# The GRU's r and z gates put into free halves of PSUM banks

## The chip, the cores and the metric

The kernel runs on one core of a Trainium2 chip. Five engines work side by side, each on its own list of instructions in order: TensorE (PE in the profile; its weight loads are PEld), VectorE (DVE), ScalarE (ACT), GpSimd (POOL) and SyncE (SP, which only issues DMAs here). They wait for one another by semaphores. There are two on-chip memories: SBUF, and PSUM with eight banks, into which TensorE writes its products. The metric is the device time of one execution in microseconds.

## The reference

A GRU runs over 128 time steps for a batch of 64 rows with 512 features, and its output is added to the input. All is float32. What one step does:

```
comb   = concat(x_t, h)
z      = sigmoid(comb @ Wz + bz)
r      = sigmoid(comb @ Wr + br)
h_cand = tanh(concat(x_t, r * h) @ Wh + bh)
h_new  = (1 - z) * h + z * h_cand
h_next = tanh(h_new @ Wp + bp)  if (t + 1) % 4 == 0 and t < T - 1  else  h_new
out[:, t] = x_t + h_new
```

The step needs the h of the step before, so the 128 steps form one chain. Only the products of x_t with the upper halves of the weights can be made ahead of time.

## The kernel before, in words

**Layout.** The state h is a tile of 128 partitions by 2 by 128. The 64 batch rows are split into two halves of 32 (index s_, the tile's middle dimension), and the 512 features into four quarters that lie on four groups of 32 partitions. A gate (`gate`, line 210) is 16 small products, each of which the profile shows as two MATMUL rows, so 32 per gate. They are written into the first half of a PSUM bank. There are three such banks, `rec_r`, `rec_z` and `rec_h` (line 154), each a tile of `[P, S, 2, J]`. Index 0 of the second dimension is the gate's own half. In `rec_r` the other half is used by the projection (`gate_ps(P_)`, line 158); in `rec_z` and `rec_h` it is free.

**One step.** In order:

1. Gate r on TensorE from the transposed state hT. Four activations on ScalarE (`crossed`, line 225; two for each half s_, as each moves 64 partitions) give r. For each half VectorE makes r*h (line 673) and transposes it into rhT (line 232). ScalarE then seeds the bank for the next step: `seed` copies the x part of the next step's gate, prepared in SBUF tile `cp`, into the gate's half of the bank, so that the next gate adds to it.
2. Gate z on TensorE, four activations, and on VectorE one instruction for keep = (z - 1) * h (line 686). Then `seed(Z, t + 1)`. In a projection step ScalarE also copies the projection's bias into `rec_r`.
3. Gate h from rhT, four tanh activations giving cand; for each half VectorE multiplies cand by z (line 718, in place), then subtracts keep to get h_new (line 728), and transposes it into hT. Then `seed(H_, t + 1)`.
4. Every fourth step a projection: a fourth gate, four tanh activations, two transposes.
5. GpSimd adds h_new to the input tile (line 794), and every fourth step SP writes four steps out.

**Work put between.** The products with x are made by a fast scheme with fewer multiplications that combines two groups of four steps at a time. It leaves TensorE a queue of units, each four small products (eight MATMUL rows), and `fill(n)` takes n units off that queue. `PLACES` (line 574), with `HEAD` and `TAIL` for the first and last steps, says how many units go ahead of gate h, after gate h, and after the projection. Some units end with work on other engines: ScalarE copies a PSUM bank to SBUF (line 468), VectorE adds a PSUM tile to an SBUF tile (lines 485 to 495), and GpSimd combines the results, by `add` (line 526) and `with_bias` (line 531), into `cp`. GpSimd also makes sums of the transposed x (lines 301 to 333). Since the batches span two groups of four steps, the schedule repeats every eight steps.

**Order and waits.** The order on each engine is the order of the program. The framework adds the waits: one instruction waits for another where they touch the same data. VectorE, ScalarE and GpSimd all take work in order, so an instruction that waits holds up what stands behind it.

Where the tiles of the change lie before: r, z and cand are SBUF tiles with two buffers each (r and cand share the tag "r"). Each of the four VectorE instructions named above (673, 686, 718, 728) thus reads two SBUF tiles.

Of the kernel before, what the change touches and what calls it, by code (L numbers as in the profile page):

```python
# [9 lines left out]
F32 = mybir.dt.float32  # L10
# [8 lines left out]
def kernel(  # L19
# [14 lines left out]
    nc = tc.nc  # L34
    B, T, D = x.shape
    H = h0.shape[1]
    P = 128
    S = 2
    V = B // S
    NQ = P // V  # L40
    J = H // NQ
# [6 lines left out]
    R, Z, H_ = range(3)  # L48
# [13 lines left out]
    two = ctx.enter_context(tc.tile_pool(name="two", bufs=2))  # L62
# [90 lines left out]

    rec = [ps_c.tile([P, S, 2, J], F32, name=f"rec_{n}") for n in "rzh"]
    P_ = 3

    def gate_ps(i):
        return rec[0][:, 1] if i == P_ else rec[i][:, 0]

# [50 lines left out]
    def gate(i, lT, w):  # L210
        for k in range(K):
            products(
                gate_ps(i), lambda h: lT[:, h, ts(k, V)], lambda c: quarters(w)[:, c, k]
            )
# [10 lines left out]
    def crossed(dst, h, ps, func):  # L225
        for d in range(2):
            nc.scalar.activation(  # L227
                dst[ts(d, 2 * V), h, :], ps[ts(h, 2 * V), d, :], func
            )

    def turn(dst, src):
        nc.vector.transpose(out=dst, in_=src)  # L232

    def new_T(tag, name):
        return two.tile([P, S, P], F32, tag=tag, name=name)
# [374 lines left out]
    for t in range(T):  # L610
# [56 lines left out]
            outer_u2(odd - 2)  # L667
        rh = two.tile([P, S, J], F32, tag="rh", name=f"rh_{t}")
        rhT = new_T("rhT", f"rhT_{t}")
        r = two.tile([P, S, J], F32, tag="r", name=f"r_{t}")  # L670
        for s_ in range(S):
            crossed(r, s_, gate_ps(R), AF.Sigmoid)
            nc.vector.tensor_mul(rh[:, s_, :], r[:, s_, :], h[:, s_, :])  # L673
# [5 lines left out]
        join(0)  # L679

        gate(Z, hT, wh[Z])
        z = two.tile([P, S, J], F32, tag="z", name=f"z_{t}")
        keep = two.tile([P, S, J], F32, tag="keep", name=f"keep_{t}")
        for s_ in range(S):
            crossed(z, s_, gate_ps(Z), AF.Sigmoid)
# [9 lines left out]
        if prop:  # L695
            nc.scalar.copy(gate_ps(P_), bias_p)
        if last:
# [13 lines left out]
        gate(H_, rhT, wh[H_])  # L711
        h_new = two.tile([P, S, J], F32, tag="h", name=f"h_{t}")
        hT = None if last else new_T("hT", f"hT_{t}")
        cand = two.tile([P, S, J], F32, tag="r", name=f"c_{t}")
        for s_ in range(S):
            c = cand[:, s_, :]
            crossed(cand, s_, gate_ps(H_), AF.Tanh)
            nc.vector.tensor_mul(c, c, z[:, s_, :])  # L718
            if last:
                o = xr[g][:, j, s_, :]  # L720
                nc.vector.tensor_add(o, c, o)  # L721
                (nc.sync, nc.scalar)[s_].dma_start(
                    out=out[ts(s_, V), t, :].rearrange("b (q n) -> q b n", q=NQ),
                    in_=o,
                )
                continue
        if not last:
            nc.vector.tensor_sub(h_new, cand, keep)  # L728
            turn(hT, h_new)
        if t < T - 2:  # L730
            seed(H_, t + 1)
# [6 lines left out]
        if prop:  # L738
            gate(P_, hT, wp)
            h = two.tile([P, S, J], F32, tag="hprop", name=f"hprop_{t}")  # L740
            hT = new_T("hT", f"hpT_{t}")
            for s_ in range(S):
                crossed(h, s_, gate_ps(P_), AF.Tanh)
                turn(hT[:, s_, :], h[:, s_, :])
# [112 lines left out]
```

## Time and profile before

| | |
|---|---|
| median of 3 runs | 1597.43 us (1591.34 to 1598.39) |
| profiled execution | 1592.18 us, span 1590.4 us |
| mean granted TensorE clock | 0.956 |
| PE busy | 1377.0 us, 87% of the span |
| DVE busy | 980.6 us, 62% |
| POOL busy | 910.1 us, 57% |
| ACT busy | 750.7 us, 47% |
| DMA | mean 40 GB/s |

How to read the lines that follow. A group row has the line, engine and operation, the tiles as out<-in, the shapes, the count, then the busy time in us with the mean of one instruction in ns, and last the idle time of the engine ahead of these instructions with what ended it. A row of the waits names who waited for whom, the total in us, how often, and the longest. A timeline row has the start in us, how long it took in us, the engine, line and operation, and in brackets the idle time of the engine before it. TensorE is called busy also where its matmuls only follow each other slowly, and its matmuls overlap, so the starts of matmuls tell more than the busy time.

### The profile page before, as it was taken

How to read it: one execution, taken by the hardware profiler on the slowest of the kernel's cores; microseconds unless marked ns; L12 is line 12 of the kernel's file. 1: busy time of each engine (PE TensorE's matmuls, PEld its weight loads, DVE VectorE, ACT ScalarE, POOL GpSimd, SP SyncE). 2: the span in 40 equal slices, each digit the busy share in tenths (PEclk: the TensorE clock that was granted, in tenths of full speed). 3: DMA queues.
4: the chain of work that ended last, by engine and by line, in shares of the span. 5: the costliest groups of instructions: out<-in, count | busy, mean ns of one | idle time of the engine just before them, and what ended most of it. 6: DMA issues, size and time to landing. Idle time of an engine off the chain costs nothing. (4 is left out here: it accounts for less than half of the span.)

```text
span 1590.4 us, 59768 instructions
## 1 busy us (share of the span) xinstructions
PE 1377.0 (87%) x26024; PEld 923.5 (58%) x26024; DVE 980.6 (62%) x1909; ACT 750.7 (47%) x2401; POOL 910.1 (57%) x1030
## 2 busy tenths in 40 slices
PE   6688898889898898898889889889898889889797
PEld 2255665656565565665656566566665656566464
DVE  0356566766757566666766666676566666666643
ACT  0134444545545454554545455455454445544444
POOL 2276665756656575666756555575666656566420
PEclk7799999999999999999999999999999999999999
DMA  2311110111111011110111111011110111111021
GB/s 99 108 55 42 33 38 16 42 42 42 29 29 48 22 42 29 48 36 16 45 38 43 29 35 49 16 42 39 46 29 20 50 29 43 29 42 29 8 83 28
DMA packets 114147, 63.13 MB, mean 40 GB/s; under 512 B 12604, under 2 KB 109116, under 8 KB 113884
## 3 DMA queue, kind: packets, MB, share of 16 engines
q1 hardware_dynamic: 113176, 58.97, 13.2%
q8 instruction: 204, 3.34, 0.9%
q14 instruction: 59, 0.48, 0.1%
q10 hardware_dynamic: 452, 0.20, 0.0%
q0 software_dynamic: 256, 0.14, 0.0%
HBM read 42.47 MB, written 16.78 MB: 37 GB/s over the span
## 5 line engine op out<-in xcount | busy, mean ns | idle before, releaser
L227 ACT ACTIVATE r<-rec_r 64x128 f32<-64x128 f32 x512 | 139.3, 272 | 411.8 <-PE rec_r L201 405.6
L201 PE MATMUL rec_h<-wh,rhT 128*32 128x256 f32 x4096 | 283.0, 381 | 53.8 <-DVE rhT L232 50.9
L201 PE MATMUL rec_r<-wh,hT 128*32 128x256 f32 x3072 | 211.5, 422 | 107.7 <-DVE hT L232 106.8
L673 DVE TENSOR_TENSOR rh<-r,h 128x128 f32<-128x128 f32 x192 | 140.5, 732 | 173.3 <-ACT r L227 173.3
L201 PEld LDWEIGHTS rec_h<-wh,rhT 128*32 128x32 f32 x4096 | 144.2, 110 | 163.2 <-DVE rhT L232 74.9
L718 DVE TENSOR_TENSOR c<-c,z 128x128 f32<-128x128 f32 x256 | 148.8, 589 | 144.7 <-ACT c L227 142.8
L227 ACT ACTIVATE c<-rec_h 64x128 f32<-64x128 f32 x512 | 139.2, 272 | 206.6 <-PE rec_h L201 200.4
L201 PEld LDWEIGHTS rec_r<-wh,hT 128*32 128x32 f32 x3072 | 103.8, 119 | 193.1 <-DVE hT L232 120.2
L526 POOL TENSOR_TENSOR cp<-mb,mb 128x768 f32<-128x768 f32 x75 | 136.1, 1815 | 119.0 <-DVE mb L495 115.4
L201 PE MATMUL rec_z<-wh,hT 128*32 128x256 f32 x3072 | 199.3, 403 | 0.0
L794 POOL TENSOR_TENSOR xr<-xr,h 128x256 f32<-128x256 f32 x127 | 93.5, 736 | 139.6 <-DVE h L728 139.6
L227 ACT ACTIVATE z<-rec_z 64x128 f32<-64x128 f32 x512 | 139.2, 272 | 51.5 <-PE rec_z L201 40.0
L526 POOL TENSOR_TENSOR mb<-mb,mb 128x768 f32<-128x768 f32 x58 | 108.5, 1870 | 91.1 <-DVE mb L495 91.1
L201 PEld LDWEIGHTS rec_z<-wh,hT 128*32 128x32 f32 x3072 | 110.5, 118 | 76.7 <-issue 23.0
L526 POOL TENSOR_TENSOR cp<-mb 128x768 f32<-128x768 f32 x47 | 88.6, 1886 | 67.6 <-ACT rec_h L369 66.1
L468 ACT COPY cq<-scratch_q 128x384 f32<-128x384 f32 (+1 forms) x214 | 102.4, 479 | 25.0 <-DVE mb L486 20.4
L686 DVE SCALAR_TENSOR_TENSOR keep<-z,h 128x256 f32<-128x256 f32 x96 | 78.7, 819 | 55.2 <-ACT z L227 55.2
L728 DVE TENSOR_TENSOR h<-c,keep 128x256 f32<-128x256 f32 x127 | 103.2, 813 | 12.4 <-DVE c L718 0.5
L531 POOL TENSOR_TENSOR mb<-mb,bias_x 128x768 f32<-128x768 f32 x35 | 64.4, 1839 | 66.6 <-DVE mb L495 66.6
L526 POOL TENSOR_TENSOR cp<-cp,mb 128x768 f32<-128x768 f32 x29 | 52.9, 1824 | 85.0 <-DVE mb L495 83.9
L232 DVE STREAM_TRANSPOSE rhT<-rh 128x128 f32<-128x128 f32 x256 | 79.7, 311 | 8.9
L201 PE MATMUL scratch_r<-tw,s 128*32 128x192 f32 x928 | 73.4, 326 | 0.0
(157 smaller groups left out, 2815.7 us busy)
## 6 DMA issues: line engine op xcount, KB each, us to landing
out_dram<-xr SPq DMA_DIRECT2D x249, 64.0 KB
xr<-in_x_dram SPq DMA_DIRECT2D x248, 64.0 KB
xs<-in_x_dram SPq DMA_DIRECT2D x240, 64.0 KB
wx<-in_L_cond_Wr_dram SPq DMA_DIRECT2D x7, 256.0 KB
wx<-in_L_cond_Wz_dram SPq DMA_DIRECT2D x7, 256.0 KB
wx<-in_L_cond_Wh_dram SPq DMA_DIRECT2D x7, 256.0 KB
wh<-in_L_cond_Wr_dram SPq DMA_DIRECT2D x4, 256.0 KB
wh<-in_L_cond_Wz_dram SPq DMA_DIRECT2D x4, 256.0 KB
```

The lines of the kernel that those rows point to most:

```text
L201: nc.tensor.matmul(ps[part(2 * h + c)], lhsT=lhs(h), rhs=rhs(c), start=start, stop=True, skip_group_check=True,)
L227: nc.scalar.activation(dst[ts(d, 2 * V), h, :], ps[ts(h, 2 * V), d, :], func)
L232: nc.vector.transpose(out=dst, in_=src)
L468: nc.scalar.copy(c[:, :nm], ps[:, :nm])
L526: nc.gpsimd.tensor_add(dst, a, b)
L531: nc.gpsimd.tensor_add(m, m, v.unsqueeze(1).to_broadcast([P, 2, 3 * J]))
L673: nc.vector.tensor_mul(rh[:, s_, :], r[:, s_, :], h[:, s_, :])
L686: nc.vector.scalar_tensor_tensor(out=keep, in0=z, scalar=1.0, in1=h, op0=ALU.subtract, op1=ALU.mult)
L718: nc.vector.tensor_mul(c, c, z[:, s_, :])
L728: nc.vector.tensor_sub(h_new, cand, keep)
L794: nc.gpsimd.tensor_add(xr[g][:, j], xr[g][:, j], h_new)
```

## The change

r and z get no SBUF tile any more: r becomes the free half of bank `rec_h`, z the free half of bank `rec_z`, one place each for all steps. ScalarE's activations for them write to PSUM. cand stays in SBUF under a tag of its own. The product with z is written over z, and the subtraction reads it from there. Each of the four VectorE instructions now has one input in PSUM and one in SBUF. Orders, counts and shapes of the instructions are the same, and so are all DMAs.

```diff
     rec = [ps_c.tile([P, S, 2, J], F32, name=f"rec_{n}") for n in "rzh"]
     P_ = 3
+    r, z = rec[H_][:, 1], rec[Z][:, 1]
...
-        r = two.tile([P, S, J], F32, tag="r", name=f"r_{t}")
         for s_ in range(S):
             crossed(r, s_, gate_ps(R), AF.Sigmoid)
             nc.vector.tensor_mul(rh[:, s_, :], r[:, s_, :], h[:, s_, :])
...
         gate(Z, hT, wh[Z])
-        z = two.tile([P, S, J], F32, tag="z", name=f"z_{t}")
         keep = two.tile([P, S, J], F32, tag="keep", name=f"keep_{t}")
...
-        cand = two.tile([P, S, J], F32, tag="r", name=f"c_{t}")
+        cand = two.tile([P, S, J], F32, tag="c", name=f"c_{t}")
         for s_ in range(S):
-            c = cand[:, s_, :]
             crossed(cand, s_, gate_ps(H_), AF.Tanh)
-            nc.vector.tensor_mul(c, c, z[:, s_, :])
+            c = z[:, s_, :]
+            nc.vector.tensor_mul(c, cand[:, s_, :], c)
...
-            nc.vector.tensor_sub(h_new, cand, keep)
+            nc.vector.tensor_sub(h_new, z, keep)
             turn(hT, h_new)
```

## The prediction

> **What bounds the kernel now.** The page comes first: its engine shares, then its costliest groups, then the list of waits, the durations of single lines, and the timeline.
>
> ```profile
> PE 1377.0 (87%) x26024; PEld 923.5 (58%) x26024; DVE 980.6 (62%) x1909; ACT 750.7 (47%) x2401; POOL 910.1 (57%) x1030
> L673 DVE TENSOR_TENSOR rh<-r,h 128x128 f32<-128x128 f32 x192 | 140.5, 732 | 173.3 <-ACT r L227 173.3
> L718 DVE TENSOR_TENSOR c<-c,z 128x128 f32<-128x128 f32 x256 | 148.8, 589 | 144.7 <-ACT c L227 142.8
> L728 DVE TENSOR_TENSOR h<-c,keep 128x256 f32<-128x256 f32 x127 | 103.2, 813 | 12.4 <-DVE c L718 0.5
> ```
> TensorE is near full, so only time in which it stands still, or runs slowly, can be won. The three VectorE rows look too dear: the list of groups kept apart by shape has 292 ns for a 128x128 product of step 0 (rh<-r,h_init).
>
> ```profile
> PE rec_r L201 <- DVE hT L232: 110.0, 39, 5.0
> PE rec_h L201 <- DVE rhT L232: 50.9, 57, 1.3
> DVE mb L491 <- ACT cq L468: 21.0, 48, 0.6
> ```
> These are rows of the waits (total, times, longest). TensorE waits on VectorE's two transposes, the ends of the two chains around each gate. The third row is needed later.
>
> ```profile
> L495 DVE TENSOR_TENSOR mb<-scratch_y,cq x53: 533/547/550, 108.5 to 1518.2; 128x384 f32<-128x384 f32 x53
> L728 DVE TENSOR_TENSOR h<-c,keep x127: 424/427/1974, 73.8 to 1577.3; 128x256 f32<-128x256 f32 x127
> L673 DVE TENSOR_TENSOR rh<-r,h x192: 248/450/1626, 81.9 to 1581.5; 128x128 f32<-128x128 f32 x192
> ```
> Single lines, minimum/median/maximum in ns. L495 adds a PSUM tile to an SBUF tile and never leaves 533 to 550. L728 and L673, two SBUF inputs, reach 1974 and 1626. The timeline shows what they meet:
>
> ```profile
> 812.64 1.95 POOL L526 TENSOR_TENSOR mb<-mb,mb 128x768 f32<-128x768 f32 x1 [4.04 <-DVE mb L495]
> 813.20 1.54 DVE L718 TENSOR_TENSOR c<-c,z 128x128 f32<-128x128 f32 x1 [0.29 <-ACT c L227]
> ...
> 814.55 1.85 POOL L531 TENSOR_TENSOR mb<-mb,bias_d 128x768 f32<-128x768 f32 x1
> 814.85 1.83 DVE L728 TENSOR_TENSOR h<-c,keep 128x256 f32<-128x256 f32 x1
> ...
> 817.22 3.35 PE L201 MATMUL rec_r<-wh,hT 128*32 128x256 f32 x32 [2.65 <-DVE hT L232]
> ```
> Each two-SBUF VectorE instruction that starts inside a GpSimd instruction ends just after it. TensorE stands 2.65 us, and then the gate takes 3.35 us where it takes 1.91 elsewhere:
>
> ```profile
> core 0: us, PE busy (x) PEld busy (x) DVE busy (x) ACT busy (x) POOL busy (x), PEclk, DMA share, GB/s
> 615.70:627.70 12.00, 9.35 (x204) 6.16 (x197) 8.45 (x15) 5.74 (x18) 7.81 (x9) 1.00 0.01 3
> 627.70:643.10 15.40, 11.64 (x212) 7.38 (x216) 10.19 (x17) 5.74 (x18) 9.25 (x10) 0.87 0.12 35
> 643.10:656.30 13.20, 13.14 (x240) 9.59 (x242) 5.69 (x16) 6.45 (x22) 5.18 (x8) 0.89 0.01 3
> ```
> After the two long stalls of a period the granted clock falls to half for 3.4 us; hence 0.87 and 0.89 over those steps.
>
> **The change, part by part.** Undisturbed durations are 292 (rh, c·z), 420 (h) and 425 ns (keep). What all instances take above these is 97.5 (rh) + 76.0 (c·z) + 49.9 (h) + 42.6 us (keep) = 266 us. With one operand in PSUM I expect this to vanish, as for L485 to L495. How much of it TensorE sees needs the steps. The schedule repeats every eight steps (u is step minus 3, modulo 8); from 211.9 to 1445.4 us it runs 13 such periods, 94.88 us each. From the timeline I took, for each u, the mean time from the first gate-r matmul to the last gate-h matmul's start, A, and from there to the next step's first matmul, B:
>
> u: A, B now -> expected
> 0: 7.70, 6.56 -> 5.75, 6.40
> 1: 6.31, 3.20 -> 6.08, 3.20
> 2: 6.28, 5.64 -> 6.28, 2.96
> 3: 8.20, 6.74 -> 6.94, 2.96
> 4: 6.67, 6.40 -> 5.75, 6.40
> 5: 7.13, 2.94 -> 7.13, 2.94
> 6: 6.46, 3.04 -> 5.75, 3.04
> 7: 7.12, 4.50 -> 5.75, 4.40
> sum: 94.89 -> 81.73
>
> How the right side comes out. A gate takes 1.73 us from its first matmul to that of the next, a queue unit 0.325 us, and 1.53 us lie between first and last start of gate h, so TensorE alone needs A = 2 x 1.73 + 0.325 x units + 1.53: 6.28 and 6.94 with 4 and 6 units (u 2, 3). With no unit or one, the chain through r decides. In the undisturbed steps 125 to 127 rhT is ready 3.80 us after the first matmul, and the last gate-h matmul starts 1.59 later.
>
> **New wait on r.** r now lies in gate h's bank. ScalarE writes its second half while VectorE would read the first. The waits row of L491 says how such a pair goes: it reads scratch_q and cx, not what the copy at L468 writes, and yet starts 33 ns after that copy (a reader of the same bank) ends. So I take it that the second pair of activations waits for the first product. Now: two activations 0.56, 0.03 to the product, 0.29, 0.31 transpose, with the second half overlapping, 1.81 in all. Then: 0.56 + 0.03 + 0.28 + 0.09 (the gap from L486 to the copy that waits for it) + 0.56 + 0.03 + 0.28 + 0.03 + 0.31 = 2.17, or 0.36 more. That gives 3.80 + 0.36 + 1.59 = 5.75 for u 0, 4, 6, 7. In u 1, after the conditional projection, r starts later (rhT ready at 4.12 in step 124) and A is 6.08. Queued behind the waiting activation on ScalarE are seed R (0.38) and z; z could start 1.93 us after gate r instead of 1.80, which keep and h outlast. The bound below is no wait: 0.36 less in these five steps, to TensorE's own limit.
>
> [...]
>
> **B.** The undisturbed chain c, product, subtraction, transpose takes 2.47 us, after 0.38 for the last matmul and 0.11 of hand-overs: 2.96. Eight units cover 0.2 + 8 x 0.325 = 2.80, so 0.16 remains of the 2.84 and 3.94 lost in u 2 and 3, and the clock no longer drops, which is the 1.26 in A of u 3 and part of u 4. In u 1 and 7 TensorE waits for ScalarE's copy of a bank (L468); that stays.
>
> **Edits costed at nothing.** keep is read from z's bank, so the copy that seeds it (seed Z) waits for keep, 0.46 us; the bias copy of a projection step and the L468 copies queue behind it. Cover: gate h's matmuls, as ScalarE sits idle 206.6 us before c (1.6 per step). Without the cover it is at most 0.46 us x 127 = 58 us. Single buffers for r and z make nobody wait: h of step t is read before gate r of t+1 can start. No DMA moves; SP's and GpSimd's orders stay. GpSimd's 58 us per period fit 81.7. **Activations into PSUM:** 128x256 copies take 377 ns into PSUM and 374 out, so 0. **c·z writes PSUM in place:** no row. Below, the 279 ns of the fastest L718; above, a second pass over 128 elements at 1.03 ns (349 to 547 ns for 192 more): 132 ns each, 0.26 us in six of eight steps, 25 us. I take 0: the nearest row, L495, shows PSUM traffic at the pace of SBUF rows.
>
> [...]
>
> **Sum.** 13 x 13.16 = 171 us. Before 211.9 us: stalls ahead of steps 2, 5, 6, 7 of 1.75 + 2.61 + 2.66 + 3.76, half-clock gates 6.2, late gates h of steps 9 and 10 2.1, less 2 for the new wait: 17. After 1445.4: 12 by the same reckoning, with 0.36 lost in each of the last five steps. Together 200. The profiled execution took 1592.18 us (span 1590.4), 0.3% under the median of 1597.43: 1392.
>
> **Rivals.**
> (a) r is not serialized: 80 steps x 0.36 = 29 us better, 1363. Against it: L491's wait.
> (b) In-place writes or PSUM activations are slower: 25 us for c·z, or 0.1 us per r activation, 0.4 x 80 = 32: 1417 to 1424.
> (c) c·z still collides, as it alone has SBUF first and PSUM second; every PSUM+SBUF row has them the other way round. Of the 13.2 us per period some 4 to 5 come back: about 1450.
> (d) The change doesn't do what it says: GpSimd delays VectorE whatever the operands. Then the 0.36 us costs 29 us, and seed Z behind the stretched keep (2.9 and 2.4 us after z in u 0 and 7) delays c by 0.5 us a period, 7 us: 1628, slower. It decides when less than a sixth of the stretch goes (36 us of cost against 200 + 29 of gross gain). Against it: L495's 550 ns maximum in a kernel with GpSimd busy 57%.
> (e) The denser schedule meets a new wait, GpSimd's cp or ScalarE's copies: half a microsecond a step, 1455.
>
> **How the numbers follow.** Mine 0.60, a 0.12, b 0.10, c 0.07, d 0.05, e 0.06. Mine alone spans 1370 to 1415 (errors of 0.15 us a step). The range leaves out d, half of c and e, and the fastest part of a: 1355 to 1450. Faster by over 0.5% (8 us, about what can be told here): 0.94; same 0.01; slower 0.05.
>
> **What would show it.** L673, L718, L728, L686 with maxima within 20% of their minima; TensorE's wait for hT from 110 to under 30 us; the clock 0.98 or more; a gap between the second and third r activation of about 0.4 us; keep ahead of seed Z. A c·z row still reaching 1.5 us means (c); all four, (d). The forecast fails if r's hand-over costs over a microsecond, or if other waits take up what VectorE gives back.

## The result, and the profile after

The changed kernel takes 1395.21 us (median of 4 runs, 1394.73 to 1395.70) where the kernel before takes 1596.33 (median of 4). The ratio is 0.8744, 95% interval 0.8723 to 0.8766. The profiled execution has a span of 1392.7 us and a mean granted clock of 0.983 (before 0.956).

The page of the changed kernel, its engine shares and the group of the r*h product. The product's mean was 732 ns:

```profile
PE 1324.7 (95%) x26024; PEld 924.6 (66%) x26024; DVE 733.7 (53%) x1909; ACT 728.3 (52%) x2401; POOL 887.4 (64%) x1030
L673 DVE TENSOR_TENSOR rh<-rec_h,h 128x128 f32<-128x128 f32 x192 | 56.0, 291 | 173.0 <-ACT rec_h L228 173.0
```

VectorE lost 247 us of busy time with the same 1909 instructions. TensorE lost 52 us with the same matmuls and stands at 95% of the span; by an estimate from the granted clocks (0.044 x 1590 us against 0.017 x 1393) up to 46 us of that come from fewer matmuls at half clock.

Single lines of the changed kernel (minimum/median/maximum ns); the lines of keep, of the product with z and of h are one lower than before, those of the helpers one higher:

```profile
L717 DVE TENSOR_TENSOR rec_z<-c,rec_z x256: 285/297/298, 73.1 to 1388.0; 128x128 f32<-128x128 f32 x128
L727 DVE TENSOR_TENSOR h<-rec_z,keep x127: 424/425/427, 74.0 to 1379.3; 128x256 f32<-128x256 f32 x127
L673 DVE TENSOR_TENSOR rh<-rec_h,h x192: 252/292/294, 82.1 to 1383.8; 128x128 f32<-128x128 f32 x192
L685 DVE SCALAR_TENSOR_TENSOR keep<-rec_z,h x96: 424/425/427, 84.5 to 1385.7; 128x256 f32<-128x256 f32 x96
```

No instance is stretched any more: the longest h takes 427 ns where it took 1974. The medians of h and keep (425 ns) are where they were (427 and 426), and that of r*h, 450 before, is now the undisturbed 292. So for these three a PSUM operand is neither faster nor slower in itself; c*z, which also writes to PSUM, takes 297 ns against 292 undisturbed.

The waits of the changed kernel:

```profile
ACT rec_z L370 <- DVE keep L685: 61.9, 126, 0.5
ACT rec_h L228 <- DVE rh L673: 47.8, 128, 2.4
PE rec_r L202 <- DVE hT L233: 16.0, 40, 1.5
```

TensorE's wait for hT fell from 110.0 to 16.0 us. The first two rows are new: ScalarE's seed of z's bank waits for keep, and its third r activation waits for the first product. In each, the two instructions touch different columns of one bank. The kernel before has neither row, and with the second half of r in another bank (below) the second row is gone.

The 13 periods, as in the prediction (A from the first gate-r matmul to the last gate-h matmul's start, B from there to the next step; measured means):

```
u   A: before  expected  after    B: before  expected  after
0       7.70     5.75     5.66       6.56      6.40     6.41
1       6.31     6.08     5.82       3.20      3.20     3.20
2       6.28     6.28     6.28       5.64      2.96     3.31
3       8.20     6.94     6.96       6.74      2.96     2.99
4       6.67     5.75     5.75       6.40      6.40     6.48
5       7.13     7.13     7.13       2.94      2.94     2.95
6       6.46     5.75     5.75       3.04      3.04     3.05
7       7.12     5.75     5.74       4.50      4.40     4.50
sum    55.87    49.43    49.08      39.02     32.30    32.89
```

The period went from 94.88 to 81.98 us (expected 81.73). Ahead of the periods 17.9 us were won (211.87 to 193.98; expected 17), behind them 12.0 (145.0 to 133.0; expected 12). The granted clock (the third value from the end) over these periods, before and then after:

```profile
211.87:1445.37 1233.50, 1092.09 (x21016) 749.69 (x21009) 806.69 (x1547) 615.20 (x1964) 757.10 (x858) 0.97 0.13 35
193.98:1259.66 1065.68, 1048.92 (x21016) 748.40 (x21008) 595.44 (x1547) 597.14 (x1964) 736.90 (x859) 1.00 0.15 41
```

### The profile page after: what moved, and what is told of

It reads as the page before. It is cut to its first block, busy times and chain, and to the rows that moved or that the text cites. A ratio compares the mean times of both kernels' runs of the same rounds, so it can differ in the third digit from the quotient of the medians.

```text
span 1392.7 us, 59942 instructions
## 1 busy us (share of the span) xinstructions
PE 1324.7 (95%) x26024; PEld 924.6 (66%) x26024; DVE 733.7 (53%) x1909; ACT 728.3 (52%) x2401; POOL 887.4 (64%) x1030
## 5 line engine op out<-in xcount | busy, mean ns | idle before, releaser
L228 ACT ACTIVATE rec_h<-rec_r 64x128 f32<-64x128 f32 x512 | 128.0, 250 | 347.7 <-PE rec_r L202 291.8
L202 PEld LDWEIGHTS rec_h<-wh,rhT 128*32 128x32 f32 x4096 | 166.0, 110 | 76.7 <-DVE rh L673 24.7
L202 PE MATMUL rec_r<-wh,hT 128*32 128x256 f32 x3072 | 184.9, 381 | 12.6 <-DVE hT L233 11.6
L202 PE MATMUL rec_z<-wh,hT 128*32 128x256 f32 x3072 | 183.8, 379 | 0.0
L228 ACT ACTIVATE c<-rec_h 64x128 f32<-64x128 f32 x512 | 139.5, 272 | 71.4 <-PE rec_h L202 64.8
L673 DVE TENSOR_TENSOR rh<-rec_h,h 128x128 f32<-128x128 f32 x192 | 56.0, 291 | 173.0 <-ACT rec_h L228 173.0
L717 DVE TENSOR_TENSOR rec_z<-c,rec_z 128x128 f32<-128x128 f32 x256 | 75.7, 296 | 131.4 <-ACT c L228 126.3
L228 ACT ACTIVATE rec_z<-rec_z 64x128 f32<-64x128 f32 x512 | 128.0, 250 | 26.9 <-PE rec_z L202 11.8
L492 DVE TENSOR_TENSOR mb<-scratch_q,cx 128x384 f32<-128x384 f32 (+1 forms) x107 | 58.1, 543 | 49.1 <-ACT cq L469 49.1
L685 DVE SCALAR_TENSOR_TENSOR keep<-rec_z,h 128x256 f32<-128x256 f32 x96 | 40.8, 425 | 79.0 <-ACT rec_z L228 79.0
L370 ACT COPY rec_z<-cp 128x256 f32<-128x256 f32 x128 | 48.2, 376 | 61.9 <-DVE keep L685 61.9
```

What stands on the lines that cost most here:

```text
L202: nc.tensor.matmul(ps[part(2 * h + c)], lhsT=lhs(h), rhs=rhs(c), start=start, stop=True, skip_group_check=True,)
L228: nc.scalar.activation(dst[ts(d, 2 * V), h, :], ps[ts(h, 2 * V), d, :], func)
L370: nc.scalar.copy(gate_ps(i).rearrange("p d (c n) -> p d c n", c=C), G[t][:, :, :, i, :].rearrange("p c d n -> p d c n"),)
L492: nc.vector.tensor_add(blocks(1, 1), runs(q_ps[:, :nm]), runs(T2[what][:, :nm]))
L685: nc.vector.scalar_tensor_tensor(out=keep, in0=z, scalar=1.0, in1=h, op0=ALU.subtract, op1=ALU.mult)
L717: nc.vector.tensor_mul(c, cand[:, s_, :], c)
```

## What holds the VectorE instruction: GpSimd's reads

The profile before showed stretched instructions beside GpSimd's, not what in GpSimd's work does it, and it left open whether PSUM as a place is simply quicker. Three kernels keep the four instructions, or the changed ones, and change GpSimd alone.

**Memsets in the kernel before.** Everything GpSimd does in the loop with x, the products and the residual becomes a memset of the same output:

```diff
     def add(dst, a, b):
-        nc.gpsimd.tensor_add(dst, a, b)
+        nc.gpsimd.memset(dst, 0.0)
```
and likewise in `four`, `sum_s12`, `sum_s34`, `with_bias` and line 794.

> The kernel before, all four instructions on SBUF tiles, but every GpSimd instruction of the loop is a memset of its output: the combinations, the sums of x and the residual addition are left out, so the time is that of a kernel without them. GpSimd writes as much as before and reads nothing. Theory (what holds a two-SBUF VectorE instruction is a GpSimd instruction that reads SBUF): rh, c*z, h and keep keep to 292, 292, 425 and 425 ns with no maximum near 1 us, no half clock in the loop, and no wait between the halves of r: about 1368 us. Rival 1 (any GpSimd instruction holds them): maxima stay in the loop and the time stays above 1430. Rival 2 (PSUM as a place is what is faster, GpSimd has nothing to do with it): about 1590.

Measured: 1352.46 us, ratio 0.8521 (0.8504 to 0.8537). Single lines of this kernel between 200 and 1250 us (671 is the r*h product, 716 the product with z):

```profile
L671 DVE TENSOR_TENSOR rh<-r,h x158: 291/292/294, 213.7 to 1245.9; 128x128 f32<-128x128 f32 x158
L716 DVE TENSOR_TENSOR c<-c,z x210: 291/292/295, 209.0 to 1241.2; 128x128 f32<-128x128 f32 x105
```

Both operands lie in SBUF, and nothing is stretched. Only ahead of 100 us, where GpSimd still adds pairs of weights, are five instances of the four instructions stretched, c*z up to 864 ns. Both rivals fall. The time is 16 us under what I had worked out; the third of these kernels shows where most of it comes from.

**Copies in the kernel before.** The same places, each a copy of one SBUF input:

```diff
     def add(dst, a, b):
-        nc.gpsimd.tensor_add(dst, a, b)
+        nc.gpsimd.tensor_copy(dst, a)
```

> The kernel before with every GpSimd instruction of the loop turned into a copy of one SBUF input (the arithmetic is left out). GpSimd still reads SBUF and waits for its inputs as before. Theory (GpSimd's reads hold VectorE's two-SBUF instructions): the maxima of rh, c*z and h stay near the length of GpSimd's longest copy plus their own, and the time stays well above that of the memsets: 1430 to 1570 us, by how long a copy takes. Rival (only GpSimd instructions with two inputs collide, or it is the arithmetic): as with memsets, about 1368.

Measured: 1391.48 us, ratio 0.8767 (0.8750 to 0.8783). Single lines of this kernel between 200 and 1250 us (ahead of 100 us GpSimd still adds pairs of weights), and GpSimd's commonest group over the whole span, in it and in the memset kernel:

```profile
L728 DVE TENSOR_TENSOR h<-c,keep x103: 424/426/859, 199.8 to 1247.5; 128x256 f32<-128x256 f32 x103
L673 DVE TENSOR_TENSOR rh<-r,h x152: 247/293/962, 215.4 to 1243.2; 128x128 f32<-128x128 f32 x152
...
L526 POOL COPY cp<-mb 128x768 f32<-128x768 f32 x122 | 109.4, 904 | 84.6 <-ACT rec_h L369 83.8
```

```profile
L524 POOL MEMSET cp<- 128x768 f32 x151 | 110.7, 739 | 101.0 <-ACT rec_h L367 100.2
```

The stretch is back, within the length of the shorter GpSimd instruction: 962 ns is 292 plus most of one copy. A memset takes almost as long as a copy (739 against 904 ns) and stretches nothing. I also counted, over the timeline's rows from 150 us on, how many of the four instructions start while a GpSimd instruction runs, and how many of those are stretched by over 40 ns:

```
kernel                  start inside one   of those stretched   stretched otherwise
before                        374                323                   0
changed                       472                  0                   0
before, memsets               156                  0                   0
before, copies                140                112                   0
```

In the kernel before, the 51 that start inside one and are not stretched all start in its last 0.2 us; with the copies 27 of 28 do, and the other one starts within 2 ns of the copy.

So the condition, as these runs show it: a VectorE instruction with two SBUF inputs was stretched beside a GpSimd instruction that reads SBUF (323 of 374 starts, and 112 of 140 with copies), not beside one that only writes (none of 156); with one of its inputs in PSUM it was not stretched beside a reading one either (none of 472).

The time is far below the 1430 expected at least and lies between that and the rival's 1368, so it decides nothing by itself; the stretched rows decide against the rival. It is so low because copies keep GpSimd busy for less of the time (33% of the span against 57%), fewer instructions start inside one, and the total stretch is 39 us against 266 before.

**Memsets in the changed kernel.**

> The changed kernel with the same memsets in place of GpSimd's work (the same parts left out). Theory: its four VectorE instructions are no longer held by GpSimd, so nothing is to be won: 1395 within 10 us, about 25 us more than the kernel before with memsets, which has no hand-over between the halves of r and no seed behind keep. Rival (GpSimd still costs the changed kernel something, through late results): 1380 or less.

Measured: 1385.55 us, ratio 0.8729 (0.8713 to 0.8746). Between 1380 and the expected 1395: at most 10 us of the changed kernel's time hang on GpSimd. The traces show most of them, and they are no stretch. In the changed kernel 110 of the 127 h have one more instruction ahead of them on VectorE, which waits for a semaphore (EVENT_SEMAPHORE, 110 rows of L727); with memsets, which do not read h, there is none. h then starts 0.40 us after the second c*z instead of 0.33, and 110 x 0.07 is 7.7 us of the 8.5 us between the two spans.

The two memset kernels are 33 us apart, where 25 had been reckoned; with the 7.7 us this gives the 16 us left open above. The 33 us are what the change costs where GpSimd stretches nothing. By the periods it is 1.61 us in A, in the five steps where r's hand-over counts, and 0.54 us in B, of which 0.34 in u 2.

## Each half of the change alone

**r alone.**

```diff
     P_ = 3
+    r = rec[H_][:, 1]
...
-        r = two.tile([P, S, J], F32, tag="r", name=f"r_{t}")
```

> Only r moves to PSUM; z, cand and the three instructions that read them stay in SBUF. Theory (each two-SBUF VectorE instruction is held by GpSimd on its own): the rh product stays at 292 ns, the c*z, h and keep instructions stay stretched (maxima near 1.9 us), and the half-clock stretches stay. Of the 12.9 us per period that the whole change won, the part ahead of gate h without the clock's share is about 5.0, net of the hand-over between the halves of r, and 2 us come in the first steps: 13 x 5.0 + 2 = 67 us, so about 1525 us. Rival (the stretch moves to whatever stays in SBUF): c*z, h and keep take more than their 168 us of stretch, and the time stays above 1560.

Measured: 1554.93 us, ratio 0.9770 (0.9754 to 0.9785).

**z alone.** The changed kernel with r back in its SBUF tile:

```diff
-    r, z = rec[H_][:, 1], rec[Z][:, 1]
+    z = rec[Z][:, 1]
...
+        r = two.tile([P, S, J], F32, tag="r", name=f"r_{t}")
         for s_ in range(S):
             crossed(r, s_, gate_ps(R), AF.Sigmoid)
```

> Only z moves to PSUM; r stays in SBUF, so nothing waits between the halves of r, and the rh product still reads two SBUF tiles. Theory: c*z, h and keep run at 296, 425 and 425 ns, TensorE's wait for hT goes and with it the half clock (granted clock 0.98), 13 x 7.9 us plus some 27 us in the first and last steps: about 1465 us. With the run that moves r alone the two gains add up to the 201 us of the whole change within 40 us. Rival (the stretch moves): the rh product takes well over its 97 us of stretch and the time stays above 1500.

Measured: 1460.81 us, ratio 0.9180 (0.9162 to 0.9197).

VectorE's groups with r alone in PSUM, then with z alone:

```profile
L718 DVE TENSOR_TENSOR c<-c,z 128x128 f32<-128x128 f32 x256 | 167.7, 665 | 121.4 <-ACT c L228 121.1
L728 DVE TENSOR_TENSOR h<-c,keep 128x256 f32<-128x256 f32 x127 | 109.8, 864 | 12.4 <-DVE c L718 0.5
```

```profile
L674 DVE TENSOR_TENSOR rh<-r,h 128x128 f32<-128x128 f32 x192 | 168.7, 878 | 142.9 <-ACT r L228 142.9
```

With z alone the forecast held. With r alone it was 30 us too low. The stretch left in SBUF was what the theory said, 164 us of 168, but it lay elsewhere: keep, whose stretch hardly counts (in the kernel before it always ends over 0.9 us ahead of the next c*z), went from 43 to 12.5 us, c*z from 76 to 95 and h from 50 to 56, and those two are on the path. In the kernel with z alone r*h went from a mean of 732 to 878 ns, and its whole stretch from 97 to 126 us. I read this so: with one chain running earlier, GpSimd's instructions meet the others at other moments. With r alone B of u 0 rose from 6.56 to 7.61 and A of u 4 from 6.67 to 8.07, the granted clock was 0.949, and only 2.6 us a period were left of the 5.0 expected. The gains alone, 37 and 131 us, sum to 168 of the 200: some 32 us belong to neither half. The rival had the direction right, not the size, and not the sum of the stretch.

These two runs also show the condition within one execution. From 150 us on, with r alone in PSUM, 172 r*h products start inside a GpSimd instruction and none is stretched, where all 101 c*z that do so are. With z alone 158 of 200 r*h are stretched, and none of 244 others.

## The price: two waits on shared banks

The hand-over in the changed kernel, ScalarE's and VectorE's rows around r in one step of u 3:

```profile
718.68 0.53 ACT L228 ACTIVATE rec_h<-rec_r 64x128 f32<-64x128 f32 x2 [2.50 <-PE rec_r L202]
...
719.24 0.29 DVE L673 TENSOR_TENSOR rh<-rec_h,h 128x128 f32<-128x128 f32 x1 [1.77 <-ACT rec_h L228]
719.56 0.54 ACT L228 ACTIVATE rec_h<-rec_r 64x128 f32<-64x128 f32 x2 [0.36 <-DVE rh L673]
...
720.13 0.29 DVE L673 TENSOR_TENSOR rh<-rec_h,h 128x128 f32<-128x128 f32 x1 [0.26 <-ACT rec_h L228]
720.46 0.31 DVE L233 STREAM_TRANSPOSE rhT<-rh 128x128 f32<-128x128 f32 x1
```

ScalarE stands 0.36 us between the two pairs, although they write other columns than VectorE reads. So the waits that the framework adds also join instructions that touch only the same bank, and not the same data. The activations are not slower for it (a mean of 250 ns, 272 before), they start later.

**r in two banks.** The second half of r goes to the free half of gate r's bank, which the projection uses only later in the step:

```diff
-    r, z = rec[H_][:, 1], rec[Z][:, 1]
+    r, z = (rec[H_][:, 1], rec[R][:, 1]), rec[Z][:, 1]
...
-            crossed(r, s_, gate_ps(R), AF.Sigmoid)
-            nc.vector.tensor_mul(rh[:, s_, :], r[:, s_, :], h[:, s_, :])
+            crossed(r[s_], s_, gate_ps(R), AF.Sigmoid)
+            nc.vector.tensor_mul(rh[:, s_, :], r[s_][:, s_, :], h[:, s_, :])
```

> The changed kernel, but the second half of r goes to the free half of gate r's own bank, so its activations do not touch the bank from which VectorE reads the first half. Theory (the 0.36 us ahead of the third r activation is a wait on the shared bank, and it sits on the path in the five steps of a period with at most one unit ahead of gate h): the 47.8 us of waiting there go, A falls by about 0.3 us in u 0, 4, 6, 7 and 0.1 in u 1, some 1.3 us per period and 0.3 in each of the last five steps: about 20 us, 1375 us. The seed of gate r's bank then waits for the second product instead, 0.1 us later than now, covered by gate z. Rival (the hand-over is hidden by TensorE's own work, or comes from something else): 1390 or more.

Measured: 1382.97 us, ratio 0.8688 (0.8674 to 0.8702). Against the same runs of the kernel before that is 0.0056 of its time, 9 us, under the changed kernel's ratio, where 20 were expected. The row of the wait is gone (gate r's seed now waits for the second product, 48.3 us in all), and A fell by 0.32 to 0.33 us in u 0, 1, 4, 6 and 7, 1.62 us in all, more than expected. But B rose by 0.32 in u 0 and 4 and by 0.13 in u 6. With gate h earlier, c's activations are ready while ScalarE is still at what stands before them:

```profile
726.71 0.38 ACT L370 COPY rec_z<-cp 128x256 f32<-128x256 f32 x1 [0.49 <-DVE keep L685]
727.02 0.37 ACT L695 COPY rec_r<-bias_p 128x256 f32<-128x256 f32 x1
727.42 0.85 ACT L228 ACTIVATE c<-rec_h 64x128 f32<-64x128 f32 x3
```

In the last two rows, of a projection step, c follows the bias copy without any idle time: ScalarE, not gate h, sets its start.

**The seed later.** In the changed kernel u 2 was the one step whose B missed the forecast. ScalarE's and VectorE's rows there:

```profile
712.09 0.43 DVE L685 SCALAR_TENSOR_TENSOR keep<-rec_z,h 128x256 f32<-128x256 f32 x1 [0.94 <-ACT rec_z L228]
712.55 0.38 ACT L370 COPY rec_z<-cp 128x256 f32<-128x256 f32 x1 [0.49 <-DVE keep L685]
712.95 0.48 ACT L469 COPY cq<-scratch_q 128x384 f32<-128x384 f32 x1
713.46 0.56 DVE L492 TENSOR_TENSOR mb<-scratch_q,cx 128x384 f32<-128x384 f32 x1 [0.94 <-ACT cq L469]
713.75 1.14 ACT L228 ACTIVATE c<-rec_h 64x128 f32<-64x128 f32 x4 [0.32 <-PE rec_h L202]
...
714.40 0.55 DVE L496 TENSOR_TENSOR mb<-scratch_y,cq 128x384 f32<-128x384 f32 x1
714.87 0.69 DVE L717 TENSOR_TENSOR rec_z<-c,rec_z 128x128 f32<-128x128 f32 x2
```

keep holds the seed, the seed the copy, the copy the three additions, and VectorE's order puts these before c*z: it starts 1.12 us after c's activations begin, where 0.58 is enough.

```diff
-        seed(Z, t + 1)
         if prop:
             nc.scalar.copy(gate_ps(P_), bias_p)
...
         fill(places[0])
+        seed(Z, t + 1)
```

> The changed kernel with the copy that seeds z's bank issued after the queue units ahead of gate h instead of before them, so that ScalarE's copies of the scratch banks no longer stand behind the wait for keep. Theory (in u 2 that wait delays the copy, the VectorE additions behind it, and through VectorE's order c*z: B is 3.31 where the chain needs 2.96): B of u 2 falls by 0.35 us, 13 x 0.35 = 4.5 us and a little in the first and last steps: about 1390 us. Rival (the wait for keep costs nothing, and B of u 2 is long for another reason): 1395, no change.

Measured: 1387.49 us, ratio 0.8719 (0.8705 to 0.8733). The ratio's interval overlaps that of the changed kernel, so the ratios alone do not settle a gain of this size; the periods do, at 81.45 us against 81.98, 13 x 0.53 = 6.9 us. The same place with the seed later:

```profile
708.83 0.48 ACT L469 COPY cq<-scratch_q 128x384 f32<-128x384 f32 x1
...
709.34 0.38 ACT L370 COPY rec_z<-cp 128x256 f32<-128x256 f32 x1
...
710.50 1.14 ACT L228 ACTIVATE c<-rec_h 64x128 f32<-64x128 f32 x4 [0.78 <-PE rec_h L202]
711.08 0.30 DVE L717 TENSOR_TENSOR rec_z<-c,rec_z 128x128 f32<-128x128 f32 x1 [0.25 <-ACT c L228]
```

B of u 2 is 2.97, and c*z comes 0.58 us after c. The projection steps won 0.08 and 0.09 us as well.

**Both edits.**

> The changed kernel with both edits: the second half of r in the free half of gate r's bank, and the seed of z's bank after the queue units ahead of gate h. Theory: with r split, c starts late in u 0 and 4 because the seed behind keep and the projection's bias copy stand before it on ScalarE; issuing that seed later takes 0.3 us off B there, 0.35 in u 2 and 0.13 in u 6: 13 x 1.1 = 14 us under the split alone, about 1369 us. Rival (the two gains overlap): 1378 to 1383.

Measured: 1368.72 us, ratio 0.8622 (0.8610 to 0.8634). The period is 80.20 us. B is back at 6.42 and 6.48 in u 0 and 4 and 2.97 in u 2, while A keeps what the split won; only u 6 keeps its 3.17. This version beats both kernels, by 13.8% the one before and by 1.2 points of ratio the changed one.

## Why the prediction was right, and where it was off

1392 was forecast and 1395.2 measured. The mechanism held; that the number is so close is in part luck, as over the 13 periods A came out 4.6 us under the forecast and B 7.7 us over it.

- **The stretch.** The step that all 266 us of it go held: none is left. That TensorE sees some 200 us held too, and 13 periods gave 167.8 of the 171.
- **The half clock.** It went with the two long stalls. In the kernel before the granted clock is 0.50 from 629.0 to 632.4 us and from 643 to 646, after the two stalls of one period. The window of the 13 periods has a granted clock of 1.00 in the changed kernel, 0.97 before. What it is worth apart from the stalls was not measured.
- **The new wait on r.** It was read off L491, a pair that only reads one bank, and it is there, for disjoint columns too: 47.8 us, a median of 0.36 us, and A came out at 5.66 to 5.75 against 5.75. In u 4, 6 and 7 the 5.75 is made of two misses that nearly cancel. From r's first activation to rhT it takes 2.09 us instead of 2.17. But r starts 0.06 us later than in the undisturbed steps, behind one more instruction on ScalarE that waits for a semaphore, although single buffers were to make nobody wait. The bound without it, rival (a) with 1363, turned out to be a version: 1368.7 with r in two banks and the seed moved.
- **The seed behind keep, costed at nothing.** This step failed. The cover named, ScalarE's idle time before c, is there (71.4 us in the changed kernel), but not in u 2: what is late is VectorE's additions behind ScalarE's copy, and they stand before c*z. Moving the seed won 6.9 us over the periods, more than the 3.2 by which the forecast missed; in u 1 the forecast was too high.
- **Activations into PSUM, costed at nothing.** An r or z activation takes 250 ns into PSUM where it took 272 into SBUF. The rows of the copies (377 and 374) did not show that, since one of the two places was SBUF in each. On r's path these are four activations, some 0.09 us a step by count, which is the 2.09 above; in u 0, where r does not start later, A shows it (5.66). u 1 came out at 5.82 instead of 6.08; 6.08 rested on one step, 124, in which r started at 2.31.
- **In place, rival (b).** c*z has a median of 297 ns against 292 undisturbed: 5 ns, not 132.
- **c*z with SBUF first, rival (c).** Its maximum is 298 ns: for this stretch it does not matter here which of the two operands lies in PSUM.
- **The change does nothing, rival (d).** 472 starts inside a GpSimd instruction and none stretched.
- **A new limit, rival (e).** ScalarE's order did become one: in the changed kernel in u 2 (the seed above), and in the version with the split for 0.1 to 0.3 us in three more steps of eight.

## What to carry to other kernels

Where a two-input VectorE instruction shows a maximum several times its minimum (here 1974 ns against 424 for h), look at what GpSimd does at that moment; if it reads SBUF, try one of the two inputs in PSUM before touching the schedule (here 1395 us instead of 1596). Then look at who else uses that bank: the program made two engines on one bank wait for each other though their columns differ (a median of 0.36 us here), and what queues behind such a wait may matter more than the wait (in u 2 a seed that waited 0.49 us put c*z 1.12 us behind the start of c, where it came after 0.58 with the seed later). And do not add up the gains of halves measured alone (37 and 131 us here, against 200 together), as a stretch that is removed in one place can move to the next (r*h went from a mean of 732 to 878 ns with z alone in PSUM).

## What had not been expected of the hardware

An activation of 64x128 float32 took 250 ns from PSUM into PSUM, also within one bank (z, `rec_z<-rec_z`: 250), and 272 from PSUM into SBUF (512 of each in one execution of the changed kernel); the two groups are r and c:

```profile
L228 ACT ACTIVATE rec_h<-rec_r 64x128 f32<-64x128 f32 x512 | 128.0, 250 | 347.7 <-PE rec_r L202 291.8 <-DVE rh L673 47.8
L228 ACT ACTIVATE c<-rec_h 64x128 f32<-64x128 f32 x512 | 139.5, 272 | 71.4 <-PE rec_h L202 64.8
```

GpSimd's memsets (739 ns in the commonest group) stretched none of the 156 VectorE instructions that started inside one, where its copies (904 ns in the commonest group) stretched 112 of 140.
